# Attention with weighted sums in quarters of the TensorE array, and a new order of TensorE's work

## The chip, the cores and the metric

The kernel runs on one core of one Trainium2 chip. The metric is device time in microseconds. The kernel before took 3394.43 us, the median of three runs (3379.18 to 3396.22). A profile comes from one further execution, whose own time is given beside its span.

## The reference

A block of four residual layers on x of 4 batches, 1024 rows and 256 columns, all in 32-bit floats: attention a, a feed-forward layer, attention b, the same feed-forward layer.

```python
x = x + attn_a(layernorm(x));  x = x + ffn(layernorm(x))
x = x + attn_b(layernorm(x));  x = x + ffn(layernorm(x))

# attn_a: 16 heads of 64
q, k, v = (einsum('bsm,hmd->bhsd', x, kernel[i]) for i in range(3))
attn = softmax(einsum('bhsd,bhtd->bhst', q, k) / (64 * 64 * 16))
out  = einsum('bhst,bhtd->bhsd', attn, v)          # then times WO

# attn_b: its own layernorm with scale and bias, a residual of its own,
# q and k, v by way of 128 columns, rotated q and k, scores / 8, softmax
c_q, c_kv = h @ w_down_q.T, h @ w_down_kv.T
q, k, v = c_q @ w_up_q.T, c_kv @ w_up_k.T, c_kv @ w_up_v.T
out = softmax(rope(q) @ rope(k).T / 8) @ v @ w_out.T + residual

# ffn: 256 -> 1024 -> 256
ffn(x) = gelu(x @ w1 + b1) @ w2 + b2
```

## The kernel before

All of x stays on the chip, in one tile per batch. Two attention stages (`attention`, lines 163 to 325) are each followed by a feed-forward stage (`ffn_between`), whose beginning is laid into the attention's last steps.

**Tiling of attention.** Work goes by pairs of heads: 4 batches x 8 pairs, and for each pair 8 steps of 128 query rows, 256 steps in a layer. A step's work is spread over several turns of the loop in `steps_with` (line 296). For step s:

- `scores` (206): TensorE multiplies q and k for both heads in 64-row by 64-column quarters of its array: head j's 64 rows of q and k lie in its half of the partitions, and `half` picks which 64 queries. Each head's scores are a tile of 128 x 1024 in PSUM, two banks; three such tiles exist (`ps_sc`).
- `exponentials` (221): per head, VectorE takes the negated maximum of each row (`nmax`), and ScalarE the exponential into `probs`, with the row sum. `probs` has 17 slabs of 128 columns: 8 slabs of keys for head 0, 8 for head 1 (`ts(j, NT)`), and a last one that holds the reciprocal sums, which `invert` (232) writes.
- `turn` (240): VectorE transposes `probs` in 32 x 32 squares into T. Two steps share one T; such a block of two steps has the number h.
- `send` (257): 16 DMAs move the squares between partition groups, so that in `pT` the keys lie on the partitions. SP issues 11 of them at the end of the odd step 2h + 1, GpSimd the other 5 in the next one.
- `weigh` (265): TensorE sums v with the weights pT. A head's 1024 keys are 8 slabs of 128 keys, each on all 128 partitions; one matmul takes a slab (128 rows, 64 columns of v) by the 256 queries of the block. `paired` (154) puts head 0 in the first, head 1 in the second half of the array's columns. Half of the slabs are taken in step s = 2h + 4 (part 0), the other half in the next (part 1), as LAG is 4.
- `divide` (275): VectorE multiplies the sums by the reciprocals into oT. `project` (284): TensorE multiplies oT with the pair's rows of the output weights (`wos`), ScalarE copies the result (`got`), GpSimd adds it to x.

**Order.** The program is in order on each engine (`manual_schedule`); it is what the loop writes. In TensorE's order a step is: scores of s + 1, in even steps project of the block before, half of weigh, then the `pieces` of that step. VectorE's order: reciprocal of s, both nmax of s + 1, in odd steps divide, turn of s. ScalarE's: the slab of reciprocals, the first exponential of s + 1, in even steps got, the second exponential. Instructions that wait hold up all that is behind them on their engine.

**Pieces.** What a pair needs ahead of its steps is cut into pieces with a step number: `qk` (496, 588) makes 512 columns of q or k, `values` (510, 609) makes v, `transposed` (140) and `down` (564) make the normalized input of a batch, `load` and `load_out` fetch weights. Layer a puts qk at 1, 3, 5, 7 and values at 5, 7, 9, 11 of the eight steps before the pair's own, all odd. In layer b, qk is followed by `rotate` a step later, on GpSimd; two DMAs issued by GpSimd fetch `turned` for it. GpSimd also issues all loads of w and wo.

**PSUM.** The small matmul groups, those of weigh included, take turns in two tiles of one bank (`ps_mm`). Together with the scores' six banks this fills PSUM.

Of the kernel before, what the change touches and what calls it, by code (L numbers as in the profile page):

```python
# [29 lines left out]
LAG = 4  # L30
NK = 2 * NT + 1
SENT = NG * HB * NK * SQ
POOL_DMA = 5
EPS = 1e-5


@with_exitstack
def hybrid_block_kernel(
# [13 lines left out]
    ps_mm = ctx.enter_context(tc.tile_pool(name="ps_mm", bufs=2, space=PSUM))  # L52
# [4 lines left out]
    lowp, highp, xnp, rp = pool("low", 2), pool("high", 2), pool("xn", 1), pool("rope", 2)  # L57
# [82 lines left out]
    def transposed(dst, src, c, affine=None):  # L140

        tr = ps_mm.tile([P, TQ, P], F32, tag="mm", name="tr")
# [20 lines left out]
    def attention(prep_batch, prep_pair, wo):  # L163
# [24 lines left out]
        def load_out(g):  # L188
            wos[g] = wop.tile([P, D], F32, tag="wo", name="wo")
            nc.gpsimd.dma_start(wos[g], wo[ts(pairs[g][1], P), :])  # L190

        for g, (b, pr) in enumerate(pairs):
# [3 lines left out]
            if g < 2:  # L196
                first.insert(g, load)
            else:
                pieces.setdefault(NT * g - NT - 4, []).append(load)
            pieces.setdefault(NT * g - 1, []).append(lambda g=g: load_out(g))  # L200
            for k, f in work:
                first.append(f) if g == 0 else pieces.setdefault(NT * g - NT + k, []).append(f)
        av = {}
# [17 lines left out]
        def exponentials(s, j):  # L221
            if j == 0:
# [3 lines left out]
            nc.vector.tensor_reduce(nmax, sc[s, j], AX.X, ALU.max, negate=True)  # L226
            nc.scalar.activation(  # L227
                probs[s][:, ts(j, NT)].rearrange("p k c i -> p (k c i)"), sc.pop((s, j)), AF.Exp,
                bias=nmax, accum_out=total[s][:, j : j + 1],
            )  # L230

        def invert(s):
            t = total.pop(s)
            nc.vector.reciprocal(t, t)  # L234
            nc.scalar.copy(  # L235
                probs[s][:, 2 * NT].rearrange("p (j c) i -> p j (c i)", j=2),
                t.unsqueeze(2).to_broadcast([P, 2, DH]),
            )
# [26 lines left out]
        def weigh(h, part):  # L265
            v = tiles[HB * h // NT]["v"]()
            if part == 0:
                av[h] = ps_mm.tile([P, HB * P], F32, tag="mm", name="av")
            half = range(part * NT // 2, (part + 1) * NT // 2)
            paired(  # L270
                av[h], [(v[:, k], [pT[h][:, :, :, j * NT + k, :] for j in range(2)]) for k in half],
                first=(part == 0), last=(part == 1),
            )

        def divide(h):
            oT[h] = otp.tile([P, HB * P], F32, tag="oT", name="oT")
            nc.vector.tensor_tensor(  # L277
                oT[h].rearrange("p (q a i) -> p a q i", a=NG, i=SQ),
                av.pop(h).rearrange("p (a q i) -> p a q i", a=NG, i=SQ),
                pT.pop(h)[:, :, :, 2 * NT, :],  # L280
# [3 lines left out]
        def project(h):  # L284
            g, t0 = divmod(HB * h, NT)
            b, pr = pairs[g]
            po = ps_mm.tile([P, HB, D], F32, tag="mm", name="po")
            for t in range(HB):
                paired(po[:, t, :], [(oT[h][:, ts(t, P)], [wos[g]] * 2)])
# [6 lines left out]
        def steps_with(others):  # L296
            for k, f in others:
                pieces.setdefault(k, []).append(f)
            for s in range(-1, n + LAG + 1):
# [4 lines left out]
                if ahead:  # L304
                    scores(s + 1)
                    exponentials(s + 1, 0)
                if part == 0 and 0 <= s // HB - 1 < n // HB:
                    send(s // HB - 1, nc.gpsimd, squares[len(squares) - POOL_DMA :])
                    T.pop(s // HB - 1)
                if part == 0 and 0 <= h - 1 < n // HB:  # L310
                    project(h - 1)
                if 0 <= h < n // HB:
                    weigh(h, part)
                if ahead:
                    exponentials(s + 1, 1)
                if part == 1 and 0 <= h < n // HB:
                    divide(h)
                if 0 <= s < n:
                    turn(s)
                if part == 1 and 0 <= s < n:  # L320
# [26 lines left out]
    def ffn(rows, store):  # L347
# [29 lines left out]
        def down(n, t):  # L377
            b, qb = blocks[n]
            if t % 2 == 0:
                po[n] = ps_mm.tile([P, 2, D], F32, tag="mm", name="po")  # L380
# [72 lines left out]
    def layer_a():  # L453
# [5 lines left out]
        def batch_a(b):  # L459
            work = []  # L460
            for qb in range(NQB):
                k = {}

                def straight(t, b=b, k=k, qb=qb):
                    if t == 0 and b == 0:
                        for i in range(TQ):
                            rows.measure(qb, i)
                        rows.finish[qb]()
                    if t == 0:
                        k["xn"] = xnp.tile([P, TQ, D], F32, tag="xn", name="xn")  # L470
                    standardize(
                        k["xn"][:, t, :], xs[b][:, qb * TQ + t, :],
# [230 lines left out]
```

## Time and profile before

| | |
|---|---|
| median of three runs | 3394.43 us |
| the profiled execution's own time | 3386.64 us |
| its span | 3384.8 us |
| instructions in the span | 69172 |
| HBM, mean over the span | 12 GB/s |
| all DMA, mean over the span | 191 GB/s |
| 128x1024 exponential, mean | 1118 ns |
| 128x1024 maximum, mean | 1214 ns |
| turn of 128x2176, mean | 2434 ns |
| median from issue to landing, squares of pT issued by SP | 4.2 us |
| the same, issued by GpSimd | 4.6 us |

Layer a's attention fills the span from about 29 to 1498 us, layer b's from about 1749 to 3150; the feed-forward stages lie between and after. A line of a profile's group names the line of the kernel, the engine and operation, the tiles written and read, their shapes, the count, then the busy time in us and the mean of one in ns, and after the second bar the time in which the engine sat idle just ahead of these instructions, with what ended it. PE is TensorE's matmuls, PEld its weight loads. A 32-bit matmul of the code leaves two matmul and two load records. In a timeline the columns are the start, the length from first start to last end, the engine and line, and how many records were merged.

### The profile page before, as it was taken

What the parts mean: (1) busy time and instruction counts of PE and PEld (TensorE: products, weight loads), DVE (VectorE), ACT (ScalarE), POOL (GpSimd) and SP (SyncE); (2) the same over time, 40 slices, a digit from 0 to 9 for tenths busy, and PEclk for the clock granted to TensorE, in tenths of its full rate; (3) what the DMA queues carried; (4) which work ended last, traced back from release to release, by engine and by line L of the source; (5) the groups of instructions that cost most, each with busy time, mean ns of one, the idle gap of its engine ahead of it and who ended that gap; (6) DMA issues with size and microseconds to landing.
All of it is one profiled execution on the core that took longest, in us unless ns stands there. A gap on an engine that the chain in (4) does not pass through costs nothing.

```text
span 3384.8 us, 69172 instructions
## 1 busy us (share of the span) xinstructions
PE 3235.4 (96%) x24960; PEld 1584.6 (47%) x24960; DVE 2594.0 (77%) x2638; ACT 1902.1 (56%) x3667; POOL 1802.1 (53%) x2546
## 2 busy tenths in 40 slices
PE   7999999999999999999999899999999998999999
PEld 3444444444444444456554444444444444444566
DVE  6988888888888888951059988888899988999200
ACT  5566565655565555543445665566656665665332
POOL 3334334343433334330258888888888978886200
PEclk9999999999999999999999999999999999999999
DMA  7877888888888888840038888888888888888200
GB/s 201 209 206 206 210 219 213 212 207 215 212 210 210 211 216 209 212 110 3 6 107 239 227 240 229 231 235 231 233 242 240 241 226 235 245 236 227 57 19 19
DMA packets 229617, 647.89 MB, mean 191 GB/s; under 512 B 74304, under 2 KB 82496, under 8 KB 229280
## 3 DMA queue, kind: packets, MB, share of 16 engines
q1 hardware_dynamic: 143696, 400.74, 46.1%
q0 software_dynamic: 85584, 242.74, 25.3%
q8 instruction: 202, 3.31, 0.4%
q14 instruction: 135, 1.11, 0.1%
HBM read 35.00 MB, written 4.19 MB: 12 GB/s over the span
## 4 chain that ended last, share of the span: by engine, by line
PE 55%; DVE 20%; issue 8%; SPq 7%; DMA 7%; ACT 2%; DVEq 1%; POOL 0%; POOLq 0%; ACTq 0%
PE sc L215 17%; PE av L158 12%; DVE nmax L226 10%; DVE T L246 9%; PE pq L158 7%; SPq L263 7%; PE po L382 7%; PE ph L371 6%; DMA pT<-T 6%; PE po L158 3%; PE pv L158 2%; DVE oT L277 1%; PE pc L158 1%; ACT p L227 1%; DVEq L246 1%
## 5 line engine op out<-in xcount | busy, mean ns | idle before, releaser
L227 ACT ACTIVATE p<-sc,nmax 128x1024 f32<-128x1024 f32 x1024 | 1144.5, 1118 | 726.3 <-DVE nmax L226 726.3
L226 DVE TENSOR_REDUCE nmax<-sc 128x1 f32<-128x1024 f32 x1024 | 1201.1, 1214 | 322.0 <-PE sc L215 320.5
L246 DVE STREAM_TRANSPOSE T<-p 128x2176 f32<-128x2176 f32 x512 | 1246.0, 2434 | 13.4 <-DMA pT<-T 4.3
L158 PE MATMUL av<-pT,v 128*64 128x256 f32 x8192 | 994.5, 385 | 92.8 <-DMA pT<-T 63.3
L263 POOL DMA_DIRECT2D pT<-T x1280 | 625.8, 496 | 782.9 <-issue 266.2
L215 PE MATMUL sc<-kT,qT 64*64 64x512 f32 x8192 | 1012.4, 603 | 7.7 <-ACT p L227 7.7
L158 PEld LDWEIGHTS av<-pT,v 128*64 128x64 f32 x8192 | 580.8, 137 | 570.8 <-issue 295.1
L215 PEld LDWEIGHTS sc<-kT,qT 64*64 64x64 f32 x8192 | 271.9, 132 | 531.1 <-issue 391.7
L294 POOL TENSOR_TENSOR x<-x,got 128x512 f32<-128x512 f32 x256 | 327.9, 1281 | 218.6 <-ACT got L292 215.2
L235 ACT COPY p<-total 128x128 f32<-128x128 f32 x512 | 152.1, 297 | 315.6 <-DVE total L234 315.4
L389 DVE TENSOR_TENSOR x<-x,po 128x512 f32<-128x512 f32 x32 | 21.9, 686 | 363.4 <-PE po L382 363.4
L158 PE MATMUL po<-wo,oT 128*64 128x256 f32 x2048 | 277.5, 392 | 0.4 <-DVE oT L277 0.4
L375 ACT ACTIVATE gT<-ph,b_sb 128x512 f32<-128x512 f32 x128 | 87.5, 686 | 306.0 <-PE ph L371 306.0
L158 PE MATMUL pq<-hT,w 128*64 128x512 f32 x1024 | 247.0, 604 | 7.9 <-DVE oT L277 4.2
L158 PEld LDWEIGHTS po<-wo,oT 128*64 128x64 f32 x2048 | 124.1, 136 | 244.0 <-issue 101.3
L382 PE MATMUL po<-w_sb,gT 128*128 128x256 f32 x1024 | 226.0, 381 | 6.2 <-ACT hT L147 6.2
L371 PE MATMUL ph<-hT,w_sb 128*128 128x512 f32 x512 | 229.8, 602 | 0.5 <-ACT hT L147 0.5
L382 PEld LDWEIGHTS po<-w_sb,gT 128*128 128x128 f32 x1024 | 193.1, 190 | 39.0 <-ACT hT L147 9.0
L227 ACT ACTIVATION_READ_ACCUMULATOR p<-sc,nmax 128x1 f32 x1024 | 201.4, 197 | 0.0
L357 POOL TENSOR_TENSOR x<-x,b_sb 128x256 f32<-128x256 f32 x64 | 44.5, 727 | 276.4 <-ACT xn L138 276.4
L606 POOL TENSOR_TENSOR turned<-turned,sin_sb 128x512 f32<-128x512 f32 x128 | 162.3, 1268 | 0.0
L371 PEld LDWEIGHTS ph<-hT,w_sb 128*128 128x128 f32 x512 | 97.1, 192 | 118.2 <-issue 112.1
(88 smaller groups left out, 2188.3 us busy)
## 6 DMA issues: line engine op xcount, KB each, us to landing
pT<-T SPq DMA_DIRECT2D x2816, 136.0 KB, 4.2
pT<-T POOLq DMA_DIRECT2D x1280, 136.0 KB, 4.6
turned<-kT POOLq DMA_DIRECT2D x128, 128.0 KB, 2.8
turned<-qT POOLq DMA_DIRECT2D x128, 128.0 KB, 3.1
w<-in_wqkv_a POOLq DMA_DIRECT2D x96, 128.0 KB, 4.9
wo<-in_wo_a POOLq DMA_DIRECT2D x32, 128.0 KB, 4.6
wo<-in_wo_b POOLq DMA_DIRECT2D x32, 128.0 KB, 3.2
out<-x SPq DMA_DIRECT2D x16, 256.0 KB, 2.1
```

Of the source, the lines that this page charges most:

```text
L158: nc.tensor.matmul(out[ts(j, DH)], lhsT[:, ts(j, DH)], rhs[j], start=(first and i == 0), stop=(last and i == len(parts) - 1),)
L215: nc.tensor.matmul(sc[s, j][ts(half, DH), ts(m, 512)], qT()[rows, ts(2 * qs + half, DH)], kT()[rows, ts(m, 512)], start=True, stop=True,)
L226: nc.vector.tensor_reduce(nmax, sc[s, j], AX.X, ALU.max, negate=True)
L227: nc.scalar.activation(probs[s][:, ts(j, NT)].rearrange("p k c i -> p (k c i)"), sc.pop((s, j)), AF.Exp, bias=nmax, accum_out=total[s][:, ...
L235: nc.scalar.copy(probs[s][:, 2 * NT].rearrange("p (j c) i -> p j (c i)", j=2), t.unsqueeze(2).to_broadcast([P, 2, DH]),)
L246: nc.vector.transpose(T[h][:, :, q, :, :].rearrange("p c k i -> p k c i"), probs.pop(s))
L263: engine.dma_start(pT[h][ts(c, SQ), a], T[h][ts(a, SQ), c])
L294: nc.gpsimd.tensor_add(xd, xd, got)
L371: nc.tensor.matmul(ph, w1_sb[:, c, ts(f, P)], hT[n][:, c, :], start=(c == 0), stop=(c == NC - 1),)
L375: nc.scalar.activation(gT[n][:, f, :], ph, AF.Gelu, bias=b1_sb[:, f : f + 1])
L382: nc.tensor.matmul(po[n][:, t % 2, :], gT[n][:, f, ts(t, P)], w2_sb[:, f, :], start=(f == 0), stop=(f == NF - 1),)
L606: nc.gpsimd.tensor_mul(turned, turned, sin_sb[:, ts(qb, QB)])
```

## The change

A head's keys now all lie in its half of the partitions: the exponentials of head j write column groups `ts(j, 2)` of 16 slabs of 64 keys each, instead of 8 slabs of their own, so that after the exchange head j's keys are on partitions 64j to 64j + 63. `weigh` runs matmuls of 64 rows by 64 columns on 128 queries: row half j by head, column half `j ^ q` by head and step q of the block, which makes four that differ in their quarter of the array. They go to the two banks of one PSUM tile `mm`; all other groups use its two halves by turns (`group`). For odd q the two heads' halves are exchanged in oT, so `wos` holds a second copy with its halves exchanged (three DMAs instead of one).

The sums of a block are taken whole, in odd steps (LAG is 5), right after a group of scores and with nothing behind them until the next scores. project and all qk, values, transposed and down pieces stand in even steps. project now comes ahead of the first exponential, divide behind turn. A number with .5 (EARLY) puts a piece ahead of weigh's place in the step, and so of the second exponential. Layer b's loads of w and wo are issued by SP. The rope pool has one buffer instead of two. v is made in slabs of 64 keys (`by_head`, 64 columns a matmul). In the prologue, the second half of the first batch is standardized by VectorE, one small exponential is run ahead of time (`ready`), and one qk and all values of the first pair move into steps -1 to 1.

```diff
-LAG = 4
+LAG = 5
+NK2 = S // DH
+EARLY = 0.5
...
-    ps_mm = ctx.enter_context(tc.tile_pool(name="ps_mm", bufs=2, space=PSUM))
+    ps_mm = ctx.enter_context(tc.tile_pool(name="ps_mm", bufs=1, space=PSUM))
+    mm = ps_mm.tile([P, 2, QB], F32, name="mm")
+    turn_of = [0]
+    def group(*shape):
+        turn_of[0] ^= 1
+        n = 1
+        for k in shape:
+            n *= k
+        flat = mm[:, turn_of[0], :n]
+        return flat if len(shape) == 1 else flat.rearrange("p (a b) -> p a b", a=shape[0])
...
-    lowp, highp, xnp, rp = pool("low", 2), pool("high", 2), pool("xn", 1), pool("rope", 2)
+    lowp, highp, xnp, rp = pool("low", 2), pool("high", 2), pool("xn", 1), pool("rope", 1)
...
+    def by_head(out, parts):
+        for i, (lhsT, rhs) in enumerate(parts):
+            for j in range(2):
+                nc.tensor.matmul(
+                    out[ts(j, DH)], lhsT, rhs[:, ts(j, DH)],
+                    start=(i == 0), stop=(i == len(parts) - 1),
+                )
...
         def load_out(g):
-            wos[g] = wop.tile([P, D], F32, tag="wo", name="wo")
-            nc.gpsimd.dma_start(wos[g], wo[ts(pairs[g][1], P), :])
+            wos[g] = wop.tile([P, HB, D], F32, tag="wo", name="wo")
+            rows = wo[ts(pairs[g][1], P), :]
+            loader.dma_start(wos[g][:, 0], rows)
+            for j in range(2):
+                loader.dma_start(wos[g][ts(j, DH), 1], rows[ts(1 - j, DH), :])
...
-                pieces.setdefault(NT * g - NT - 4, []).append(load)
-            pieces.setdefault(NT * g - 1, []).append(lambda g=g: load_out(g))
+                pieces.setdefault(NT * g - NT - 3 - EARLY, []).append(load)
+            pieces.setdefault(NT * g - 1 - EARLY, []).append(lambda g=g: load_out(g))
...
+            place = j ^ (s % HB)
             nc.scalar.activation(
-                probs[s][:, ts(j, NT)].rearrange("p k c i -> p (k c i)"), sc.pop((s, j)), AF.Exp,
-                bias=nmax, accum_out=total[s][:, j : j + 1],
+                probs[s][:, :NK2, ts(j, 2), :],
+                sc.pop((s, j)).rearrange("p (k c i) -> p k c i", c=2, i=SQ), AF.Exp,
+                bias=nmax, accum_out=total[s][:, place : place + 1],
             )
...
-        def weigh(h, part):
+        def weigh(h):
             v = tiles[HB * h // NT]["v"]()
-            if part == 0:
-                av[h] = ps_mm.tile([P, HB * P], F32, tag="mm", name="av")
-            half = range(part * NT // 2, (part + 1) * NT // 2)
-            paired(
-                av[h], [(v[:, k], [pT[h][:, :, :, j * NT + k, :] for j in range(2)]) for k in half],
-                first=(part == 0), last=(part == 1),
-            )
+            for k in range(NK2):
+                for q in range(HB):
+                    for j in range(2):
+                        nc.tensor.matmul(
+                            mm[ts(j ^ q, DH), q, :P], v[ts(j, DH), k, :],
+                            pT[h][ts(j, DH), :, q, k, :],
+                            start=(k == 0), stop=(k == NK2 - 1),
+                        )
...
-                paired(po[:, t, :], [(oT[h][:, ts(t, P)], [wos[g]] * 2)])
+                paired(po[:, t, :], [(oT[h][:, t], [wos[g][:, t]] * 2)])
...
                 if ahead:
                     scores(s + 1)
-                    exponentials(s + 1, 0)
-                if part == 0 and 0 <= s // HB - 1 < n // HB:
+                if part == 1 and 0 <= s // HB - 1 < n // HB:
                     send(s // HB - 1, nc.gpsimd, squares[len(squares) - POOL_DMA :])
                     T.pop(s // HB - 1)
-                if part == 0 and 0 <= h - 1 < n // HB:
-                    project(h - 1)
-                if 0 <= h < n // HB:
-                    weigh(h, part)
+                if part == 1 and 0 <= h < n // HB:
+                    project(h)
+                if ahead:
+                    exponentials(s + 1, 0)
+                for f in pieces.get(s - EARLY, ()):
+                    f()
+                if part == 0 and 0 <= h < n // HB:
+                    weigh(h)
                 if ahead:
                     exponentials(s + 1, 1)
-                if part == 1 and 0 <= h < n // HB:
-                    divide(h)
                 if 0 <= s < n:
                     turn(s)
-                if part == 1 and 0 <= s < n:
+                if part == 0 and 0 <= h < n // HB:
+                    divide(h)
+                if part == 0 and 0 <= s < n:
                     send(s // HB, nc.sync, squares[: len(squares) - POOL_DMA])
...
-            work = [(5 - 4 * i + 2 * qb, lambda i=i, qb=qb: qk(i, qb)) for i in (1, 0) for qb in range(NQB)]
-            work += [(5 + 2 * m, lambda m=m: values(m)) for m in range(NT // 2)]
+            work = [(6 - 4 * i + 2 * qb - EARLY, lambda i=i, qb=qb: qk(i, qb)) for i in (1, 0) for qb in range(NQB)]
+            work += [(6 + 2 * m, lambda m=m: values(m)) for m in range(NT // 2)]
...
+        first = loads + [lambda: measured(0)] + xn[:4] + [lambda: measured(1), ready] + xn[4:6] + pair[:1]
+        first += xn[6:] + pair[1:3]
+        later += [((-1, 0, 0, 1, 1)[i], f) for i, f in enumerate(pair[3:])]
...
-                    nc.gpsimd.dma_start(w[:, i], up[:, ts(pr, P)])
+                    nc.sync.dma_start(w[:, i], up[:, ts(pr, P)])
...
-                    k = 3 - 4 * i + 2 * qb
-                    work += [(k, lambda i=i, qb=qb: qk(i, qb))]
+                    k = 4 - 4 * i + 2 * qb
+                    work += [(k - EARLY, lambda i=i, qb=qb: qk(i, qb))]
                     work += [(k + 1, lambda i=i, qb=qb: rotate(i, qb))]
-            work += [(5 + 2 * qb, lambda qb=qb: values(qb)) for qb in range(NQB)]
+            work += [(4 + 2 * qb, lambda qb=qb: values(qb)) for qb in range(NQB)]
```

## The prediction

> **What bounds the kernel now.** I read the page's busy line first, then the windows view of a steady stretch of each attention layer, the groups, and last TensorE's own timeline, because 96% busy says only that some matmul was in flight.
>
> ```profile
> PE 3235.4 (96%) x24960; PEld 1584.6 (47%) x24960; DVE 2594.0 (77%) x2638; ACT 1902.1 (56%) x3667; POOL 1802.1 (53%) x2546
> ```
> ```profile
> 51.21:55.86 4.65, 4.43 (x24) 0.97 (x20) 4.65 (x7) 3.11 (x6) 0.00 (x0) 1.00 1.03 268
> ...
> 300.00:1100.00 800.00, 796.83 (x6882) 374.80 (x6880) 694.82 (x643) 480.59 (x954) 312.64 (x497) 1.00 0.82 212
> 2000.00:3000.00 1000.00, 938.09 (x7772) 428.05 (x7770) 888.75 (x820) 613.07 (x1191) 837.06 (x1108) 0.99 0.87 235
> ```
>
> The windows' columns are PE, PEld, DVE, ACT, POOL busy, clock, DMA share, GB/s. Layer A (300 to 1100) is TensorE's: 797 of 800. In layer B (2000 to 3000) TensorE idles 6%, with DVE at 89%, DMA at 87%, GpSimd at 84%. The first window is a step of the fill, with VectorE busy throughout: 4.65 us, its shortest step.
>
> I count in blocks of two steps (one h, 256 query rows of a head pair); there are 128 per layer. A block has 32 score records (a matmul of the code leaves two). Layer B had 2912 in its 1000 us: 91 blocks of 10.99 us. For A, a block line by line:
>
> ```profile
> 648.04 1.95 PE L215 MATMUL sc<-kT,qT 64*64 64x512 f32 x16
> 649.91 1.95 PE L158 MATMUL av<-pT,v 128*64 128x256 f32 x16
> 651.69 1.89 PE L158 MATMUL pq<-hT,w 128*64 128x512 f32 x8
> 653.41 1.04 PE L158 MATMUL pv<-w,hT 128*64 128x128 f32 x16
> 654.38 1.95 PE L215 MATMUL sc<-kT,qT 64*64 64x512 f32 x16
> 656.26 1.08 PE L158 MATMUL po<-wo,oT 128*64 128x256 f32 x8
> 657.38 1.95 PE L158 MATMUL av<-pT,v 128*64 128x256 f32 x16
> 659.26 1.95 PE L215 MATMUL sc<-kT,qT 64*64 64x512 f32 x16
> ```
>
> Starts tell more than durations, which overlap. The block is 659.26 - 648.04 = 11.22 us. Records start together in twos (128*64, two column halves) or fours (64*64, four quarters): one pass. Start to start, a pass takes 0.429 us with 512 columns (pq: 4 passes, 1.72), 0.216 with 256, 0.109 with 128. A prologue stretch shows the last at length, 32 passes in 3.64 us with a change of form at its end:
>
> ```profile
> 25.08 3.71 PE L158 MATMUL pv<-w,hT 128*64 128x128 f32 x64
> 28.72 1.52 PE L215 MATMUL sc<-kT,qT 64*64 64x512 f32 x12
> ```
>
> Four score passes need 1.72 us, yet the next group starts 1.87 to 1.88 later, and av's 8 passes (1.73) take 1.78 before pq. Each change between 64*64 and 128*64 costs about 0.11 before the new group and 0.05 in its first pass: **0.16 us**, four times a block. A second loss stands between po and av: 1.12 us for 0.86 of passes and 0.05 of first pass, leaving 0.21; there TensorE's queue goes through the many semaphores of pT's DMAs. In layer B they are also late:
>
> ```profile
> 2328.63 1.08 PE L158 MATMUL po<-wo,oT 128*64 128x256 f32 x8
> 2330.73 1.95 PE L158 MATMUL av<-pT,v 128*64 128x256 f32 x16 [1.02 <-DMA pT<-T]
> ```
> ```profile
> PE av L158 <- DMA pT<-T: 39.3, 34, 3.2
> ```
>
> (second fence: the waits of 2000 to 3000; us, times, longest).
>
> **What the skill says.** TensorEngine Tiling (Array Packing), Key Properties: a change of tiling mode drains TensorE, a change of tile alone does not. The trace agrees: 0.16 us at each change, none between av and pq. The same page, Gotcha 1: PSUM Pressure: row tiles write different PSUM banks and can't use one bank at once. The scores keep to it (each head has its own banks); no line of before shows two row halves in one bank. TensorE: Matmul & The Clock Gate, "Wait — 56ns, not 53.3ns?": matmul starts are never under about 25 ns apart however few columns, and 62 ns where firmware decodes. The prologue's 64 are 54.5 ns apart on average, so 62 is excluded; scores of one pass start 7 ns apart, nearer than the stated floor. Runtime: NRT & Kernel Launch, Instruction fetch mechanics: a sequencer's floor is about 20 cycles an instruction. I price that below.
>
> **The change, part by part.**
>
> *Weighted sums in quarters.* Per block, 16 matmuls of 128 rows by 256 columns become 64 of 64 rows by 128 columns: 32 records become 128, in fours. 32 passes of 0.109 are 3.49 us against 16 of 0.216, 3.46: +0.03. That pv does 0.109 with two 64-column loads a pass, and scores run four quarters with four loads, is the nearest evidence; the combination is not shown. Below, 3.46 is the floor (the same array work); above, the rivals' 4.27 and 6.98. I take 3.49.
>
> *Order.* sums stand between two score groups of the same form, everything else in the other gap: four changes a block become two, -0.32 us. The po-to-av loss (0.21) goes too, since the semaphores are now passed behind 1.7 us of scores; I leave 0.10 of waiting.
>
> *Layer A*: scores 3.43 + sums 3.49 + po 0.86 + pq 1.72 + values 0.90 + two changes 0.32 = 10.72, plus 0.06 for transposes and 0.10 of waits: 10.88. Against 11.22 that is -0.34, times 128: **-44 us**. VectorE's block is 2 x 4.65 + 0.41 (oT) = 9.71 and hides under it.
>
> *LAG 5.* The sums come one step later, some 5 us more for pT to land. In B this removes most of 39.3/91 = 0.43 us a block. What is late next: VectorE (888.75/91 = 9.77 a block), TensorE (10.88 less half of pq and of values, plus 0.28 for the down-projections and B's transposes: about 9.85), DMA (0.87 x 10.99 = 9.56) and SP, all within 3%. Such near-equal chains never mesh wholly: before, the largest was about 9.95 + waits of 1.04. I keep 0.6 and take 10.45: -0.54 x 128 = **-69 us**; bounds 10.05 and 10.95.
>
> *Values.* 128 columns become 64 a matmul, twice as many. If a pass falls to half of 0.109 this is level (I add 0.03); if weight loads stop that, it stays 0.109: +0.87 us a block in A, half in B, +167 us together at worst. Since pv's loads already hide beneath passes of 0.109, I take little, and leave the end to the rivals.
>
> *Moved DMAs.* In B, per four blocks, three w issues and one wo issue leave GpSimd (4 x 0.57 = 2.3 us of 44, at 84% busy) and six issues join SP. SP issues 11 pT squares a block, 0.5 to 1.4 us each, some 8.9 us of 11, then waits 1.7 to 2.4 us for the turned T. The six (3.6 us) are placed ahead of that wait, so two blocks of four lose their cover of about 1.8 us and shift later squares by some 0.3, which LAG 5 absorbs. In A, two more wo issues (2 x 0.58) fall on a GpSimd 39% busy: nothing. With one rope buffer the next DMA into `turned` stands behind the rotation on GpSimd's own queue anyway: nothing.
>
> *ScalarE.* `got` (0.58) now stands ahead of the first exponential. Queued behind it are that exponential and the scores that need its buffer: up to 0.3 us in B's even steps, inside the 0.6 kept. VectorE's divide now follows the turn (2.43); TensorE needs it only after the next scores (1.9), and is by then 3.5 us of sums further: covered, by a few tenths. The exponential's stores in runs of 64 I cost at nothing: ScalarE is 56% busy.
>
> *One psum tile in two halves*: the same two banks by turns: nothing. *Prologue*: one q/k group (1.72) and all values (3.64) move behind the first scores, where TensorE idles in VectorE's steps, and the exponential's table load (1.28) moves earlier: -7. *One more step of lag* at each layer's fill and end: +2.5 each. Together **-2**.
>
> Sum: -44 - 69 - 2 = -115. Against the profiled execution's 3386.6 (span 3384.8): 3271.6, say **3270**. That execution lies 0.2% under the runs' median of 3394.4, within their 0.5% spread; I add nothing.
>
> **Rivals.**
>
> *The waits stay* (given back). VectorE or SP becomes the bound in B, and A saves only its switches less new stalls: -25 in A, -10 in B: 3350. For: four chains within 3% in B. Against: the late DMAs are named, and A has slack on every other engine.
>
> *Supply of instructions (slower).* A quarter pass has 4 loads and 4 matmuls in 109 ns, 13.6 ns each; the densest steady stretch before, pv, is 27. At the Runtime page's 20 cycles of the 1.2 GHz that the TensorE page gives a sequencer, 16.7 ns (an estimate), the 256 records take 4.27 us: +0.78 x 256 = +200, so 3470. It decides from 115/256 = 0.45 us a block, 15.4 ns a record. For: doubled density for 3.5 us on end. Against: starts 7 ns apart in scores, and a queue that fills behind them.
>
> *The quarters don't run side by side*: both row halves write one bank at once. Passes double to 6.98 us: +893, 4165. Against: within each half of the partitions the two writers are in different banks.
>
> **Numbers.** Forecast 0.73 (its own range 3200 to 3345), waits stay 0.12, supply 0.10, quarters 0.05. Range 3200 to 3390. Half a per cent is about what a measurement of this kernel can tell from no change: faster 0.81 (0.73 + 0.08), same 0.04, slower 0.15.
>
> **What would show it.** av records 32768, in fours 109 ns apart, 3.5 us a block between scores with no gap; po straight after the other scores; A's block at 10.9, B's near 10.45; av's DMA wait near zero; VectorE in B over 92% busy. Fours 130 ns or more apart would prove the supply rival, 218 the bank one; blocks unchanged with sums at 3.5 the first.

## The result and the profile after

The changed kernel takes **3848.14 us**, the median of four runs (3841.80 to 3851.67), beside 3386.85 for the kernel before (now four runs as well): a ratio of 1.136 (95% interval 1.132 to 1.140). It is 13.6% slower, where the forecast was 3270. The profiled execution took 3841.8 us, its span 3840.0.

The page of the kernel after answers first, with the busy line and the groups of TensorE. In a group the last figure of the line is the idle time just ahead of it, with its releaser.

```profile
PE 3309.7 (86%) x52608; PEld 1980.9 (52%) x52608; DVE 2627.7 (68%) x2642; ACT 1919.9 (50%) x3664; POOL 1765.6 (46%) x2482
...
L243 PE MATMUL sc<-kT,qT 64*64 64x512 f32 x8192 | 1056.3, 615 | 96.7 <-POOL qT L654 85.6
...
L301 PE MATMUL mm<-pT,v 64*64 64x128 f32 x32768 | 962.6, 271 | 10.0 <-issue 7.1
...
L172 PE MATMUL mm<-hT,w 128*64 128x512 f32 x1024 | 251.4, 612 | 92.6 <-ACT got L324 90.5
...
L181 PE MATMUL mm<-w,hT 128*64 128x64 f32 x4096 | 147.8, 225 | 91.6 <-ACT qT L539 43.2
L172 PE MATMUL mm<-c,w 128*64 128x512 f32 x512 | 138.1, 618 | 91.4 <-ACT got L324 91.4
```

TensorE was busy 96% of the span and is now at 86%; no engine took its place, each is idle more than before. The sums (L301), the heart of the change, wait for almost nothing: 10.0 us in the whole span, DMAs included. Other groups wait instead: those of L172 and L181 for ScalarE's copies (`got`, `qT`), the scores for GpSimd's rotation (`qT L654`). The windows view shows the same by stage; its columns are those of the table before.

```profile
300.00:1100.00 800.00, 705.93 (x12988) 416.78 (x12982) 624.35 (x564) 423.45 (x836) 294.75 (x473) 1.00 0.72 189
2000.00:3000.00 1000.00, 836.85 (x14951) 499.77 (x14950) 787.36 (x736) 551.00 (x1050) 683.14 (x886) 0.96 0.80 209
```

In layer a, where TensorE had 797 busy of 800, it has 706, and VectorE fell from 695 to 624. TensorE's timeline there, one block and a little more:

```profile
652.87 1.95 PE L243 MATMUL sc<-kT,qT 64*64 64x512 f32 x16
654.64 3.67 PE L301 MATMUL mm<-pT,v 64*64 64x128 f32 x128
658.13 1.90 PE L243 MATMUL sc<-kT,qT 64*64 64x512 f32 x16
659.96 1.08 PE L172 MATMUL mm<-wo,oT 128*64 128x256 f32 x8
661.78 1.94 PE L172 MATMUL mm<-hT,w 128*64 128x512 f32 x8 [0.74 <-ACT got L324]
664.41 1.15 PE L181 MATMUL mm<-w,hT 128*64 128x64 f32 x32 [0.69 <-ACT kT L541]
665.49 1.95 PE L243 MATMUL sc<-kT,qT 64*64 64x512 f32 x16
```

Read the starts. The 128 quarter records take 658.13 - 654.64 = 3.49 us, 109 ns a pass, with no gap on either side. But the q/k group (L172, `mm<-hT,w`) starts 1.82 us after project, whose four passes need 0.86, and the values (L181) 2.63 after q/k, whose four need 1.72. Each waits until ScalarE has copied out the group *ahead* of it, though that group lies in the other half of `mm`. The block is 12.62 us. In layer b there is a second stall; first GpSimd's timeline, then TensorE's, at the step in which a new pair's scores begin:

```profile
2597.78 1.29 POOL L326 TENSOR_TENSOR x<-x,got 128x512 f32<-128x512 f32 x1
2599.00 1.11 POOL L647 DMA_DIRECT2D turned<-qT  x2
2603.64 1.25 POOL L652 TENSOR_TENSOR qT<-qT,cos_sb 128x512 f32<-128x512 f32 x1 [3.54 <-DMA turned<-qT]
...
2606.19 1.26 POOL L654 TENSOR_TENSOR qT<-qT,turned 128x512 f32<-128x512 f32 x1
```
```profile
2607.51 3.36 PE L243 MATMUL sc<-kT,qT 64*64 64x512 f32 x16 [3.68 <-POOL qT L654]
```

GpSimd issues the DMA into `turned` and has nothing else queued but the rotation that waits for it, so it stands idle for 3.54 us. TensorE pays twice: it stops for 3.68 us, and the score group behind the stop takes 3.36 us where the others take 1.95. The windows view from this group's start to the next group's shows why; the third figure from the end is the granted clock, as a share of full speed:

```profile
2607.51:2610.70 3.19, 3.19 (x16) 1.05 (x20) 0.00 (x0) 0.00 (x0) 3.17 (x6) 0.54 0.92 247
```

The clock was about half, and it is back at 1.00 in a window from 2611 on. Over 2000 to 3000 it averages 0.96, which is worth at most 0.04 of a block, some 0.5 us (an estimate from these figures; in part of the slow time TensorE was idle).

Before the change, the issue came in an odd step, and GpSimd's send and its add filled the time until the rotation in the next one (the add is among the lines left out):

```profile
2307.70 1.06 POOL L600 DMA_DIRECT2D turned<-kT  x2 [1.35 <-ACT kT L598]
2309.06 2.44 POOL L263 DMA_DIRECT2D pT<-T  x5 [0.30 <-issue]
...
2313.81 1.27 POOL L605 TENSOR_TENSOR kT<-kT,cos_sb 128x512 f32<-128x512 f32 x1
```

### The profile page after: what moved, and what is told of

The parts are those of the page before. It is cut to its first block, busy times and chain, and to the rows that moved or that the text cites. A ratio compares the mean times of both kernels' runs of the same rounds, so it can differ in the third digit from the quotient of the medians.

```text
span 3840.0 us, 124243 instructions
## 1 busy us (share of the span) xinstructions
PE 3309.7 (86%) x52608; PEld 1980.9 (52%) x52608; DVE 2627.7 (68%) x2642; ACT 1919.9 (50%) x3664; POOL 1765.6 (46%) x2482
## 4 chain that ended last, share of the span: by engine, by line
PE 31%; DMA 6%; POOL 6%; DVE 5%; ACT 3%; SPq 3%; issue 3%; DVEq 0%; POOLq 0%; ACTq 0%
PE sc L243 8%; PE mm L417 6%; PE mm L301 6%; PE ph L406 6%; PE mm L172 4%; SPq L293 3%; DMA pT<-T 3%; DVE T L276 2%; DMA turned<-qT 2%; POOL pT L293 2%; DVE nmax L254 2%; DMA turned<-kT 1%; ACT got L324 1%; POOL x L326 1%; POOL turned L653 1%
## 5 line engine op out<-in xcount | busy, mean ns | idle before, releaser
L301 PEld LDWEIGHTS mm<-pT,v 64*64 64x64 f32 x32768 | 941.7, 134 | 158.2 <-issue 142.0
L301 PE MATMUL mm<-pT,v 64*64 64x128 f32 x32768 | 962.6, 271 | 10.0 <-issue 7.1
L172 PE MATMUL mm<-hT,w 128*64 128x512 f32 x1024 | 251.4, 612 | 92.6 <-ACT got L324 90.5
L172 PE MATMUL mm<-wo,oT 128*64 128x256 f32 x2048 | 277.9, 392 | 12.6 <-DVE oT L309 10.9
L324 ACT COPY got<-mm 128x512 f32<-128x512 f32 x256 | 149.8, 585 | 232.4 <-PE mm L172 224.3
L417 PE MATMUL mm<-w_sb,gT 128*128 128x256 f32 x1024 | 235.1, 388 | 26.7 <-DVE x L424 13.0
L172 PEld LDWEIGHTS mm<-wo,oT 128*64 128x64 f32 x2048 | 124.4, 136 | 257.8 <-DVE total L264 164.8
L181 PEld LDWEIGHTS mm<-w,hT 128*64 128x64 f32 x4096 | 130.1, 138 | 202.2 <-ACT qT L539 97.8
L417 PEld LDWEIGHTS mm<-w_sb,gT 128*128 128x128 f32 x1024 | 195.3, 193 | 66.6 <-DVE x L424 19.1
L181 PE MATMUL mm<-w,hT 128*64 128x64 f32 x4096 | 147.8, 225 | 91.6 <-ACT qT L539 43.2
L172 PE MATMUL mm<-c,w 128*64 128x512 f32 x512 | 138.1, 618 | 91.4 <-ACT got L324 91.4
```

The lines of the kernel that those rows point to most:

```text
L172: nc.tensor.matmul(out[ts(j, DH)], lhsT[:, ts(j, DH)], rhs[j], start=(first and i == 0), stop=(last and i == len(parts) - 1),)
L181: nc.tensor.matmul(out[ts(j, DH)], lhsT, rhs[:, ts(j, DH)], start=(i == 0), stop=(i == len(parts) - 1),)
L301: nc.tensor.matmul(mm[ts(j ^ q, DH), q, :P], v[ts(j, DH), k, :], pT[h][ts(j, DH), :, q, k, :], start=(k == 0), stop=(k == NK2 - 1),)
L324: nc.scalar.copy(got, po)
L417: nc.tensor.matmul(po[n][:, t % 2, :], gT[n][:, f, ts(t, P)], w2_sb[:, f, :], start=(f == 0), stop=(f == NF - 1),)
```

## The experiments

Two theories came out of these views. **Theory 1**: the one PSUM tile `mm`, of which each half waits for the reader of the other. **Theory 2**: GpSimd's new order in layer b. The later expectations say for themselves which theories they set against each other. For every run the stages were measured in the trace, from the starts of the scores (in us; a layer's time from its first to its last score record, over 128 blocks; the last column is some 3.2 us short of the span's end in every row):

| kernel | first scores | a: block | a to b | b: block | after b's last scores | span |
|---|---|---|---|---|---|---|
| before | 28.7 | 11.18 | 262.4 | 10.96 | 256.1 | 3384.8 |
| after | 29.2 | 12.68 | 293.9 | 12.58 | 279.8 | 3840.0 |
| e1 two tiles | 22.3 | 10.90 | 264.9 | 12.65 | 258.5 | 3563.4 |
| e2 send later | 28.3 | 12.76 | 295.2 | 11.76 | 278.5 | 3744.0 |
| e3 both | 22.4 | 10.94 | 266.0 | 11.21 | 259.0 | 3386.4 |
| e4 before, shared | 38.7 | 16.23 | 294.9 | 14.79 | 281.1 | 4587.2 |
| e11 earlier pair | 21.9 | 10.89 | 265.3 | 10.87 | 258.1 | 3334.2 |
| e12 the same, wide | 22.3 | 10.96 | 263.8 | 10.57 | 258.1 | 3302.8 |

**e1: two tiles for the halves.** The change with `mm` as two tiles of a bank each; divide, which read both halves at once, becomes two instructions.

```diff
-    mm = ps_mm.tile([P, 2, QB], F32, name="mm")
+    mm = [ps_mm.tile([P, QB], F32, tag=f"mm{i}", name=f"mm{i}") for i in range(2)]
...
-        flat = mm[:, turn_of[0], :n]
+        flat = mm[turn_of[0]][:, :n]
```

> The changed kernel with the shared PSUM tile split into two tiles of one bank each (the divide becomes two instructions of 128x128). Theory 1 (a group's first matmul waits for the reader of the group before, although that lies in the other half of the same tile): the 1.77 us a block that TensorE waits for ScalarE's copies go, layer A's block falls from 12.62 to about 10.9 us (-223 us), the feed-forward stages give back about 55. With theory 2 added (layer B is also held by GpSimd, which now sits idle between issuing the turned DMAs and the rotation right behind them), B's block stays at 12.2 or more and the whole is near 3520; without theory 2, B falls too and the whole is near 3350. If the waits were only slack of another limit, the time stays near 3848.

Measured: 3566.51 us, ratio to before 1.052 (1.050 to 1.054). TensorE's timeline in layer a:

```profile
658.67 1.95 PE L243 MATMUL sc<-kT,qT 64*64 64x512 f32 x16
660.44 3.67 PE L301 MATMUL mm<-pT,v 64*64 64x128 f32 x128
663.94 1.90 PE L243 MATMUL sc<-kT,qT 64*64 64x512 f32 x16
665.76 1.08 PE L172 MATMUL mm<-wo,oT 128*64 128x256 f32 x8
666.68 1.89 PE L172 MATMUL mm<-hT,w 128*64 128x512 f32 x8
668.39 1.10 PE L181 MATMUL mm<-w,hT 128*64 128x64 f32 x32
669.42 1.95 PE L243 MATMUL sc<-kT,qT 64*64 64x512 f32 x16
```

Same instructions, same order, same TensorE work: q/k now starts 0.92 after project (1.82 with one tile), the values 1.71 after q/k (2.63), and the block is 10.75 instead of 12.62. Theory 1 holds for layer a and for both feed-forward stages, which got back 29 and 21 us. But layer b did not move: 12.65. Its granted clock fell a little further, to 0.94 of full speed in 2000 to 3000. There GpSimd holds it, as the waits of 2000 to 3000 say (us, times, longest):

```profile
POOL kT L654 <- DMA turned<-kT: 175.1, 40, 5.8
...
POOL qT L654 <- DMA turned<-qT: 125.7, 39, 5.9
...
PE sc L243 <- POOL qT L656: 114.1, 19, 8.2
```

**e2 and e3: GpSimd's send behind the DMA of `turned`.** e2 is the change with the send moved; e3 is e2 with the two tiles of e1.

```diff
                 if part == 1 and 0 <= h < n // HB:
                     project(h)
...
                 for f in pieces.get(s - EARLY, ()):
                     f()
+                if part == 1 and 0 <= s // HB - 1 < n // HB:
+                    send(s // HB - 1, nc.gpsimd, squares[len(squares) - POOL_DMA :])
+                    T.pop(s // HB - 1)
```

> The changed kernel with one move alone: GpSimd's five pT DMAs are issued behind the pieces with .5, so that they stand between the issue of turned and the rotation. Theory 2 says that GpSimd's wait for turned in layer B (about 3 us a block) shrinks, but as the shared tile still costs TensorE 1.77 us a block, B's block only falls from 12.58 to 12.4 or so and A's stays at 12.62: 3800 to 3850 in all. If GpSimd were the one limit of B, B would fall to about 11 and the whole to 3650.

> Both edits: two PSUM tiles and the later send. Theories 1 and 2 together: A's block 10.9, B's 10.4 to 10.8, feed-forward stages as before the change, 3270 to 3330 in all, faster than the kernel before. If something else holds B (LAG, SP's added loads, the order on ScalarE), B stays above 11.5 and the whole above 3430.

Measured: e2 3745.73 us in one run; e3 3385.75, ratio 1.000 (0.998 to 1.001). In e2 layer b's block fell from 12.58 to 11.76, more than was expected, with layer a as it was. Part of that, at most the 0.5 us estimated above, is the clock: with the stops gone it averages 1.00 in 2000 to 3000, in e2 and in e3. With both edits b is at 11.21. So b has two obstacles, and each hides part of the other: the two tiles bring b nothing while GpSimd is late (12.58 to 12.65), and 0.55 once it isn't (11.76 to 11.21). e3 removes the whole loss and no more, so its expectation of 3270 to 3330 was missed: b stays 0.25 over before. Its waits of 2000 to 3000 show what is left:

```profile
DVE T L276 <- DMA pT<-T: 58.2, 39, 2.8
...
POOL kT L654 <- DMA turned<-kT: 50.5, 39, 2.6
```

VectorE's turn waits for the squares of T to be sent, and GpSimd sends its five later; before, the row read `DVE T L246 <- DMA pT<-T: 2.7, 4, 1.6`. In e1, where the send had kept its place and GpSimd was late for other reasons, it was 40.2 already, so the moved send is only a part of it.

**e4: the old kernel with the shared tile.** The kernel before, its small groups in the halves of one tile by the `group` of the change; nothing else is touched.

```diff
-                av[h] = ps_mm.tile([P, HB * P], F32, tag="mm", name="av")
+                av[h] = group(HB * P)
...
-            po = ps_mm.tile([P, HB, D], F32, tag="mm", name="po")
+            po = group(HB, D)
```

> The kernel before with one part of the change alone: its two PSUM tiles of ps_mm become the two halves of one tile, used by turns as before. Theory 1: sums wait for the copy of the projection, q/k for the divide, values for the q/k copy, 0.8 us or more each, some 1.5 to 2.7 us a block that little can hide in layer A: 3387 rises to between 3750 and 4100. If halves of one tile are told apart, nothing changes: 3387.

Measured: 4589.0 us in one run, 35% over before and well over what was expected. TensorE's timeline in layer a:

```profile
709.86 1.08 PE L168 MATMUL mm<-wo,oT 128*64 128x256 f32 x8
712.97 3.05 PE L168 MATMUL mm<-pT,v 128*64 128x256 f32 x16 [2.03 <-ACT got L302]
...
718.36 1.95 PE L168 MATMUL mm<-pT,v 128*64 128x256 f32 x16
721.23 1.09 PE L168 MATMUL mm<-w,hT 128*64 128x128 f32 x16 [0.93 <-DVE oT L287]
```

The tile alone does it, and in the old order it costs more (5.0 us a block against 1.8): after project the sums wait for `got`, which ScalarE takes behind an exponential, and the next group waits for VectorE's divide of the sums. Part is again the clock: behind the stop of 2.03 us the 16 records of the sums take 3.05, further on 1.95, and the clock averages 0.93 over 300 to 1100 (at most 0.07 of a block, some 1.1 us, by the same estimate). In the change's order the tile costs less; which part of the order does that was not tested.

**e5 and e6: the rotation a block later.** e5 is e1 with `rotate` a whole block behind its DMA; e6 is e5 with layer b's w and wo loads issued by GpSimd again.

```diff
-                    work += [(k + 1, lambda i=i, qb=qb: rotate(i, qb))]
+                    work += [(k + 2 - EARLY, lambda i=i, qb=qb: rotate(i, qb))]
```

> Two PSUM tiles, GpSimd's five pT DMAs back at their early place, and each rotation of layer B moved to the next even step, just ahead of the next q/k group, so that a whole block lies between the issue of turned and its use. Theory 2 (GpSimd's order is what held B) with the addition that the later send of the run before this one made the turn wait for T: both waits go, B's block falls from 11.2 to about 10.4 or 10.5, the whole from 3386 to about 3290. If layer B is instead held by what the DMA engines and SP can move, B stays at 11.0 or more and the whole at 3360 or more.

> The kernel of e5_rotate_later with layer B's loads of w and wo issued by GpSimd again (three wo DMAs a pair, as in the change). If SP's six added loads a pair delay the squares and with them T's release, this is faster than e5 by 20 us or more and the turn waits less for DMA. If GpSimd's queue is the limit, it is slower by up to 70 us (six issues of 0.57 us per four blocks). If neither, within 10 us of e5.

Measured: 3510.9 us (1.036, 1.034 to 1.038) and 3510.3 (1.036). The expectation of e5 was missed: the waits for `turned` went and VectorE's wait for T fell to 3.3 us in 1000, but b's block only fell from 12.65 to 12.22 and the clock stayed at 0.95, because the pair's first scores still stalled, as in e1 (119.0 us by the same row). q's first half was rotated in the step directly before them:

```profile
PEld sc L243 <- POOL qT L656: 91.5, 20, 7.4
```

Where the loads are issued makes no difference here, so SP's six further issues are not what holds layer b in e5.

**e7 and e8: two parts of the change by themselves.** e7 is e5 with sums, v and wo in the old wide form (128 rows, 64 columns), whole, at the change's place between two groups of scores. e8 is e5 with the first exponential ahead of project again.

```diff
+                    exponentials(s + 1, 0)
                 if part == 1 and 0 <= h < n // HB:
                     project(h)
-                if ahead:
-                    exponentials(s + 1, 0)
```

(the diff is e8's.)

> The kernel of e5_rotate_later with the sums as before in 128 rows by 64 columns, 256 queries (and keys, values, wo and divide laid out as before), but still whole and between two groups of scores. What the quarters themselves are worth: two more changes of form a block, 0.29 us net. Where TensorE is the limit that is +37 us in layer A, and up to as much again in B: slower than e5 by 30 to 75. If a change of form cost nothing that counts, the time equals e5 or is lower by the saved wo loads.

> The kernel of e5_rotate_later with the first exponential of a step ahead of the projection again, as before the change. If ScalarE's copy ahead of the exponential holds the score tiles, faster than e5 by 10 to 40 us, in B above all; as forecast (its cost lies inside other waits), within 10 us of e5; it can also be slower, as the copies that free the small PSUM tiles then come later.

Measured: e7 3495.53 us (1.032), e8 3613.39 (1.067). e8 is 102 us slower than e5, and a block of layer a takes 11.42 instead of 10.91: with two tiles, ScalarE's new order, copies first, is worth that much. Of e8's expectations only the last, slower, came true. e7's timeline in layer a tells what the quarters are worth at their place:

```profile
659.69 1.95 PE L241 MATMUL sc<-kT,qT 64*64 64x512 f32 x16
661.57 3.67 PE L172 MATMUL mm<-pT,v 128*64 128x256 f32 x32
665.17 1.95 PE L241 MATMUL sc<-kT,qT 64*64 64x512 f32 x16
667.05 1.08 PE L172 MATMUL mm<-wo,oT 128*64 128x256 f32 x8
...
669.68 1.04 PE L172 MATMUL mm<-w,hT 128*64 128x128 f32 x16
670.66 1.95 PE L241 MATMUL sc<-kT,qT 64*64 64x512 f32 x16
```

From scores to sums it is 1.88 us and from sums to scores 3.60, against 1.77 and 3.49 or 3.50 with quarters (e1 and the change), and 1.88 against 1.82 after the second scores. That is 0.28 more; with the 0.03 by which quarter sums were reckoned longer, two changes of form cost 0.31 together. The values give back 0.05 (0.98 with 128 columns, 1.03 with 64), and the block is 10.97 against 10.75. The median block over the layer is 10.96 against e5's 10.80, so 0.17 of the expected 0.29 shows; the means are nearer, 10.95 against 10.91, as the quarter sums take longer in some blocks. Yet e7 as a whole is 15 us faster than e5, where 30 to 75 slower was expected: the quarter form costs more in layer b (12.22 against 12.08) than it brings in a.

**e9 and e10: `turned` fetched by ScalarE's queue.** e9 is e1 with ScalarE issuing the two DMAs behind its copy; e10 has the wide form of e7, and two rope buffers.

```diff
-                    nc.gpsimd.dma_start(turned[r::2], straight[1 - r :: 2])
+                    nc.scalar.dma_start(turned[r::2], straight[1 - r :: 2])
```

> e1 (two accumulators for the halves), and the two DMAs that fill turned are issued by ScalarE, directly behind its copy of q or k, instead of by GpSimd behind its send and its add; the rotation stays where the change put it. Theory 1 (what is left of layer B's loss is GpSimd's order alone: the DMA is issued late on a queue that then waits for it): the rotation finds its data landed, GpSimd's waits for turned (139.5 us in 800) fall under 20, B's block falls from 12.65 to 10.6 or less, no turn waits for T's squares since the send isn't moved, whole 3290 to 3320, faster than before. Theory 2 (VectorE and the squares' DMAs bind B once GpSimd is free, as the waits of e3 hint): B's block stays at 11.2, whole about 3385. If GpSimd's remaining work (send, add, rotation in series behind late inputs) binds for itself: B over 12, whole over 3480.

> The same on ScalarE's queue, with the sums and values in the old wide form (whole, between two groups of scores, as in e7), whose single wo loads leave room for two rope buffers as before the change: ScalarE's issue then never waits for the rotation before. If the single rope buffer matters (ScalarE stalls at the issue until the rotation is done and the exponentials behind it come late), B is shorter here than in e9 by 0.3 us or more, against 0.17 us a block that the wide form costs in TensorE-bound layer A: whole 3290 to 3320 beside an e9 of 3340 or more. If it doesn't, this one is about 0.17 x 128 + 0.1 x 128, some 20 to 35 us slower in A and B, offset by up to 15 us of wo loads: 0 to 25 us slower than e9.

Measured: 3659.88 us (1.082, 1.078 to 1.086) and 3612.9 (1.069): theories 1 and 2 of e9 both missed. Its numbers lie in the range of the third case (b's block is 13.20), but not for that cause. ScalarE's timeline in e9 shows why:

```profile
2534.31 0.60 ACT L647 ACTIVATE qT<-mm 128x512 f32<-128x512 f32 x1
2534.98 1.81 ACTq L649 DMA_DIRECT2D turned<-qT  x2
2536.84 1.11 ACT L256 ACTIVATE p<-sc,nmax 128x1024 f32<-128x1024 f32 x1 [1.93 <-issue]
...
2537.95 0.58 ACT L620 COPY c<-mm 128x512 f32<-128x512 f32 x1
```

The issue holds ScalarE's queue for 1.1 to 1.8 us in its fullest step (four such steps of this timeline), and the second exponential and the copies behind it come late by as much. GpSimd gained little, with 224 us of waiting for `turned` in 800 (e1: 301 in 1000): copy, flight of the DMA and rotation are as close together as ever, whichever queue issues. e10's block in b is 0.24 shorter than e9's, no more than the wide form brings by itself between e11 and e12 below, so nothing shows that the second rope buffer helped. e10 was 47 us faster than e9, which neither of its cases had.

**e11 and e12: the pair's q and k one block earlier.** e11 is e5 with layer b's q/k groups and down-projections two steps earlier, and w loaded three earlier. e12 is e11 in the wide form.

```diff
-                work += [(2 * NT + 6 + 4 * (1 - i) + 2 * qb, lambda i=i, f=down: f(i)) for i in (1, 0)]
+                work += [(2 * NT + 4 + 4 * (1 - i) + 2 * qb, lambda i=i, f=down: f(i)) for i in (1, 0)]
...
-                    k = 4 - 4 * i + 2 * qb
+                    k = 2 - 4 * i + 2 * qb
```

> e5 (two accumulators for the halves; the rotation one block after its DMA, so that GpSimd never waits for turned), and layer B's q, k and down-projections made one block earlier (with w's load three steps earlier), so that the late rotation of q's first half no longer stands just before the pair's first scores. Theory 1 (layer B's loss beside the accumulators is when GpSimd gets to the rotation, and no engine is short of time): the stall of 9 to 12 us at each pair's first scores goes, B's block falls from 12.2 to between 10.5 and 10.8 with hardly any wait for turned or for T's squares, whole 3290 to 3330, faster than before. Rival (B is bound by VectorE and the squares' DMAs in any order): B stays at 11.2, whole about 3385. If q and k take turns with something else not seen yet: above 3450.

> e11 with the sums, values and wo loads in the old wide form, whole between two groups of scores. If the quarter form pays at its place (0.17 us a block in layer A, between e5 and e7): 10 to 25 us slower than e11. If its doubled wo loads and lower-half stores cost layer B as much as it saves in A, as e7 against e5 hints (15 us the other way, with the stalls of both in it): equal within 10 us, or faster than e11.

Measured: **e11 3336.05 us, 0.985 (0.982 to 0.987); e12 3303.81, 0.975 (0.973 to 0.977)**. e12 is faster than the kernel before; e11's gain of 1.5% is small but clear of the interval. GpSimd's timeline in e11:

```profile
2604.09 1.14 POOL L649 DMA_DIRECT2D turned<-kT  x2 [0.30 <-POOL qT L656]
2606.61 2.44 POOL L293 DMA_DIRECT2D pT<-T  x5 [1.38 <-DVE total L264]
2609.30 1.27 POOL L328 TENSOR_TENSOR x<-x,got 128x512 f32<-128x512 f32 x1 [0.25 <-ACT got L326]
2610.54 1.27 POOL L654 TENSOR_TENSOR kT<-kT,cos_sb 128x512 f32<-128x512 f32 x1
```

The rotation finds its data landed, as it did before the change, and no score waits for GpSimd. The clock is back at 1.00. b's block is 10.87, so the rival (11.2 in any order) falls, though theory 1's 10.5 to 10.8 and 3290 to 3330 were just missed. e12's windows view of layer b shows TensorE busy nearly throughout again, with VectorE at 935:

```profile
2000.00:3000.00 1000.00, 991.79 (x8078) 447.54 (x8078) 935.40 (x869) 634.19 (x1236) 827.74 (x1060) 1.00 0.92 245
```

Busy isn't pace, though: waits between the records of one group count as busy. In e12's timeline one score group of a block in layer b is followed after 2.34 us (2592.92 to 2595.26), the other after 1.88 (2598.86 to 2600.74).

Of e12's expectations the last came true: it is 32 us faster than e11. Quarters cost layer b 0.30 us a block (10.87 against 10.57). The groups of 2000 to 3000 show where part of it lies, e11 first, then e12:

```profile
L301 PE MATMUL mm<-pT,v 64*64 64x128 f32 x11776 | 381.4, 270 | 15.0 <-issue 11.4 <-DMA pT<-T 0.3 <-ACT hT L163 0.3
```
```profile
L172 PE MATMUL mm<-pT,v 128*64 128x256 f32 x3040 | 349.0, 382 | 0.0
```

At 128 and 32 records a block these are 92 and 95 blocks, so the quarter sums are busy for 4.15 us a block and the wide ones for 3.67, which is what either form takes in layer a's timelines. In e11's trace the sums of layer b still run at 109 ns a pass; the excess stands for the most part between the first passes of a group, and the profile doesn't name what they wait for. GpSimd's waits that are put down to wo's loads (13.2 us, against 8.0 in e12; the loads are twice as large in quarters) are too little for the whole. The cause stays open.

## Why the prediction was wrong, step by step

The forecast is 570 us short, span against span. Layer a's blocks account for (12.68 - 10.88) x 128 = 230, layer b's for (12.58 - 10.45) x 128 = 273, the feed-forward stages beyond the longer lag for 50, the fill ahead of the first scores for 8. The 9 us that are left come from the base: the forecast read blocks of 11.22 and 10.99 in steady stretches, and the layers' means before are 11.18 and 10.96.

- **"One psum tile in two halves: the same two banks by turns: nothing" failed**, and it is the largest error: the step priced the banks and not the waits. With one tile, the next group's first matmul waits for the last read of the tile, in whichever half. e1 took this away and e4 put it in alone: both ways it is shown. It costs 0.90 and 0.92 us at two places in a block of layer a, 29 and 21 us in the feed-forward stages, and 7 of the fill.
- **"With one rope buffer the next DMA into `turned` stands behind the rotation … nothing" failed** for another reason than the buffer. The step asked what the DMA waits for, not what waits for the DMA. q/k had moved into the even step, behind GpSimd's send and add, which had been the cover of the DMA's flight. e2 shows the price with one tile (12.58 to 11.76), e11 with two (12.65 to 10.87, over 200 us of the whole). Both prices hold the slow clock behind the stops, which no part of the prediction had.
- **Layer a's sum was right.** Without the shared tile its block is 10.90 on average, against 10.88 forecast. Its steady block of 10.75 meets the 10.72 summed ahead of transposes and waits, and the 0.16 of a change of form is met by the 0.31 that two of them cost in e7.
- **Sums in quarters and values were right for the changed kernel**: 3.49 us for 32 passes, as taken; 1.03 for the values with their change of form, 58 ns a pass. The rivals on supply (130 ns or more) and on the bank (218) are refuted by the 109. Once layer b's stops are gone the sums there take more than the 3.49: 4.15 busy a block in e11, beside 3.67 in layer a.
- **LAG 5 was right in direction.** TensorE's wait for pT's DMAs is 0.3 us in 1000 in e11 (39.3 before), beside 11.4 ahead of the sums that the trace puts down to issue. But no run changes LAG alone, so that the lag did it is not shown. Layer b's 10.45 was too good: 10.87 in e11, 10.57 in e12. The lag's own price agrees: the stages behind the two layers are 2.5 and 2.4 us longer in e1 than before, where 2.5 each was forecast.
- **ScalarE's order was priced from the wrong side.** The step looked for what copies first would cost (up to 0.3 us, hidden) and not for what they bring: in e8 going back to the old order costs 102 us. **SP's loads at about nothing** held in e6. The fill was right too once the tile is split: -6.4 us against -7.
- **The rivals.** None of the three was it. The two on the slow side were sought in TensorE's own pace, and the time lay in what TensorE was made to wait for.

## What to carry to other kernels

When buffers are merged into one tile, list for each writer the last reader of *every* part of that tile: a wait goes by the tile that the program names, and two disjoint halves can serialize like one buffer. When an instruction is moved on an in-order queue, find what ran between a DMA's issue and its first use; if the move takes that cover away, move the use as well, by as much as the flight is long. Look at the granted clock behind a long stop of TensorE as well: there a stop cost more than its own length. And try both repairs at once: in layer b the first alone was worth nothing.

## What the runs showed of the hardware

- Two row halves of the array wrote one PSUM bank at once, in different halves of its partitions, at full pace: the four quarters start 6 or 7 ns apart, and the next four 109 ns after the first. The Trainium skill, TensorEngine Tiling (Array Packing), Gotcha 1: PSUM Pressure, says that different row tiles can't access one bank simultaneously; here the measurement decides otherwise for disjoint partitions.
- 128 quarter matmul records in 3.49 us are 27 ns each, with their loads 13.6 ns an instruction, held through the groups of the changed kernel's timeline in layer a.
- A matmul of 64 columns in two column halves makes passes of 58 ns (1.03 us for 16, less 0.11 for the change of form), so with half the columns and twice the passes a group took only 0.05 us longer.
- Two DMAs issued by ScalarE held its queue for 1.1 to 1.8 us; GpSimd's took 1.1.
- Behind stops of 2.03 us (e4) and 3.68 us (the change) TensorE's next group had a granted clock of 0.62 and 0.54: its 16 records took 3.05 and 3.36 us instead of 1.95. How long a stop must be for that was not measured.
